# A graph-attention and FFN block on one core: one more projection by Strassen's algorithm, three mask columns in flight, and a bias moved

## The chip, the cores and the metric

The kernel runs on one core of a Trainium2 chip. The core has a matrix engine (TensorE, PE in the profile, with PEld for the loading of weights), a vector engine (VectorE, DVE), an activation engine (ScalarE, ACT), GpSimd (POOL) and SyncE (SP), which here only issues transfers. Transfers issued by one engine form a queue. The metric is device time in microseconds, the median of several runs.

## The reference

For x of 384 rows (nodes) and 1024 features:

```
h  = layernorm(x)
q  = h @ wq.T + bq;  k = h @ wk.T + bk;  v = h @ wv.T + bv
q2 = q @ wiq.T + biq; k2 = k @ wik.T + bik; v2 = v @ wiv.T + biv   # 16 heads of 64
mask = full(-inf); mask[src, dst] = softplus(etw)[type - 1]         # 12288 edges, the last one wins
mask[i, i] = softplus(etw)[3] where no edge is
a  = softmax(q2 @ k2.T / 8 + mask) @ v2                             # by head
x  = x + a @ wo.T + bo
h  = layernorm(x)
h  = silu(h @ w1 * s1) * (h @ w2 * s2);  h = gelu(h @ h1 * t1);  h = gelu(h @ h2 * t2)
x  = x + h @ w3 * s3
```

All weights of the attention are 1024 x 1024 in float32. The rows of a softmax sum to one, so a bias added to v2 comes out of the attention as the same bias.

## The kernel before

**Layout.** Activations are kept transposed where they are the input of a projection: xT, qT, vT, kT, q2T, k2T and aT have 8 tiles of 128 features by 384 nodes. v2 is kept with nodes in partitions (3 row tiles of 128 x 1024). Weights come as two halves of 2 MB each (512 output features), four buffers in all. A half's load can be issued only when the last product that reads the buffer's former contents is done. SP issues all of these loads and the other small ones in program order: a transfer that waits holds up all behind it.

**Order of work.** TensorE, VectorE, ScalarE and SP take their instructions strictly in the order in which the program names them; only GpSimd is left to the scheduler. The stages are: layernorm and transposes; q by plain matmuls (`project`, L378); q2, v and k by one level of Strassen's algorithm in the Winograd form (`project_fast`, L435); v2 by plain matmuls (L502 to L515); then k2 woven into the attention by heads (L556 and on), the output projection wo (L540), and the FFN.

**Strassen.** The weight is cut into quarters b11, b12, b21, b22 (b11 and b21 in the first half, b12 and b22 in the second) and the input into a11 to a22 (features by nodes). Four sums s1 to s4 of the input (`row_sums`) and four of the weight are made on VectorE: t3 = b22 - b12 (`third`, its own tile), b12 - b11 (`first`), then b11 + t3 (L459) and b21 minus that, all of them but t3 in place, 128 x 2048 elements each. Seven products m1 to m7 replace eight. The order on TensorE is: b11 with a11, t3 with s3, the new b11 with s2 (the third product), b21 with a12, b12 with s1, b22 with s4, the new b21 with a22. The call `beside[i]()` lets other work stand between the products in program order; `beside[0]` stands after the first product and ahead of b11 + t3.

**The mask table.** The edges are 96 columns of 128. A scatter (L355) writes one column's values into a table in DRAM, with an indirect transfer from GpSimd. So that the last edge wins, an entry whose cell occurs again later in the window of columns that can be in flight together is sent to a spare cell (`targets`, L333, on VectorE: for each column, a comparison of its keys with the keys of that and the following columns). DEEP = 2 columns are in flight: scatter i waits for scatter i - 2. `chunk()` does eight columns: it issues the load of the next eight columns' keys (`keys`, kr, on SP), makes the targets of its own eight, and issues eight scatters. After the last scatter the table is read back into nmask (L517), which the first step after the scores (L591, with the row's largest value) reads.

**Other places the change touches.** GpSimd adds the output bias bo to the residual xs after that (L523). The attention's product with v2 goes through a copy on ScalarE into aT (L621). For the FFN's weights the kernel tests whether they have low bits (`inspect`, L180, on ScalarE, sixteen pieces); the flag goes through a small matmul (L712) and a branch. `row` holds broadcast rows: biv and bo first, later the FFN's last scale in biv's place.

Of the kernel before, what the change touches and what calls it, by code (L numbers as in the profile page):

```python
# [30 lines left out]
DEEP = 2  # L31
# [12 lines left out]
def gnn_ffn_kernel(ctx: ExitStack, tc: tile.TileContext, x, edges, etw, vecs, rows,  # L44
# [34 lines left out]
    def load_rows(at, first, n):  # L79
        nc.sync.dma_start(row[:, at:at + n, :], bass.AP(  # L80
            tensor=rows.tensor, offset=rows.offset + first * F, ap=[[0, P], [F, n], [1, F]]))
# [98 lines left out]
    def inspect(raws):  # L180
        for raw in raws:
# [5 lines left out]
            nc.scalar.activation(low, low, AF.Copy, accum_out=lows[:, at:at + 1])  # L187
# [5 lines left out]
    with tc.tile_pool(name="edge", bufs=1) as ep, tc.tile_pool(name="krow", bufs=2) as krp, \  # L193
# [4 lines left out]
        tab = dram.tile([CELLS + DEEP * P, 1], FP, name="tab")  # L198
# [4 lines left out]
        for t in range(NT):  # L203
# [5 lines left out]
        nc.gpsimd.iota(spare, pattern=[[0, CHUNK // DEEP], [P, DEEP]], base=CELLS,  # L209
                       channel_multiplier=1, allow_small_or_imprecise_dtypes=True)  # L210
# [121 lines left out]

        def targets(c0, krf):  # L333

            for j in range(CHUNK):
                c = c0 + j
                w = min(DEEP, NCOL - c) * P
# [15 lines left out]
        def scatter(c0):  # L353
            for c in range(c0, c0 + CHUNK):
# [3 lines left out]
                for other in sent[-DEEP + 1:]:  # L358
                    tc.declare_no_dep(i, other, reason="no cell in common")
                if len(sent) >= DEEP:  # L360
                    after(i, sent[-DEEP])
# [34 lines left out]
        def row_sums(src, tag):  # L396

            sums = act.tile([P, 4, HK, HN], FP, tag=tag, name="sums")
            s1, s2, s3, s4 = (sums[:, i] for i in range(4))
            (a11, a12), (a21, a22) = ([src[:, k:k + HK, r:r + HN] for k in (0, HK)]  # L400
                                      for r in (0, HN))
# [10 lines left out]
        def third(at=0):  # L412

            b11, b12, b21, b22 = blocks(at)
            t3 = tp.tile([P, HK, FH], FP, tag="t3", name="t3")
            minus(t3, b22, b12)
            return t3
# [17 lines left out]
        def project_fast(src, sums, t3, dst, bias, beside):  # L435
# [3 lines left out]
            a11, a12, a22 = src[:, :HK, :HN], src[:, HK:, :HN], src[:, HK:, HN:]  # L439
# [41 lines left out]
        with tc.tile_pool(name="third", bufs=1) as tp, \  # L481
# [6 lines left out]
            sums_x = row_sums(xT, "k2T")  # L488
            chunk()
            load_rows(0, 0, 2)  # L490
# [4 lines left out]
            sums_q = row_sums(qT, "v2")  # L495
            t3s = []
            project_fast(qT, sums_q, t3, q2T, vec[:, BIQ:],
                         [nothing, chunk, chunk, lambda: t3s.append(third(2))])
            vT = act.tile([P, KF, N], FP, tag="t", name="vT", bufs=2)
            project_fast(xT, sums_x, t3s[0], vT, vec[:, BV:], [first, chunk, chunk, chunk])  # L500
            v2 = act.tile([P, NT, F], FP, tag="v2", name="v2")
            for half in range(2):  # L502
                (w,) = queue.pop(0)
                c = slice(half * FH, (half + 1) * FH)
                for t in range(NT):
                    ps = ps_st.tile([P, 512], FP, tag="st", name="ps")
                    for k in inputs:
                        nc.tensor.matmul(ps, lhsT=vT[:, k, t * P:(t + 1) * P], rhs=w[:, k, :],  # L508
                                         start=k == inputs[0], stop=k == inputs[-1])
                    nc.vector.tensor_add(v2[:, t, c], ps, row[:, 0, c])  # L510
                prefetch()
                for _ in range(2 - half):
                    chunk()
                if half == 0:
                    t3 = third(1)  # L515
            load_rows(0, 2, 1)
# [4 lines left out]
            for t in range(NT):  # L521
                tc.keep_in_program_order(
                    nc.gpsimd.tensor_add(xs[:, t, :], xs[:, t, :], row[:, 1, :]))  # L523
            kT = act.tile([P, KF, N], FP, tag="t", name="kT", bufs=2)
            project_fast(xT, sums_x, t3, kT, vec[:, BK:], [first, nothing, nothing, nothing])
# [6 lines left out]
    ps_ff = ctx.enter_context(tc.tile_pool(name="ps_ff", bufs=4, space=bass.MemoryType.PSUM))  # L532

# [16 lines left out]
    with tc.tile_pool(name="attn", bufs=1) as ap, \  # L550
# [62 lines left out]
        def weighted(pair):  # L613
# [7 lines left out]
            nc.scalar.copy(aT[:, pair, :], av[:, :N])  # L621
# [85 lines left out]
    for t in range(NT):  # L707
        st = small.tile([P, 2, 6], FP, name="st")
        add_out(multiply_out(t, 0), t, 0, st)
        if t == 2:  # L710
            fl = ps_mm.tile([P, 512], FP, tag="mm", name="fl")
# [3 lines left out]
            transpose_x2(1)  # L715
# [161 lines left out]
```

## Time and profile before

| | us |
|---|---|
| median of three runs (410.71 to 413.0) | 411.58 |
| the profiled execution | 408.51 |
| its span, first to last instruction | 406.5 |
| TensorE busy / VectorE / ScalarE / GpSimd | 389.9 / 211.4 / 106.3 / 123.3 |
| L508, v2's matmuls, 96 records, mean 0.592 each from start to end | 41.4 busy |
| L355, 96 scatters: busy, and idle before them | 108.0, 112.7 |
| of that idle, waiting for an earlier scatter to land | 66.2 |

A float32 matmul stands in the trace as two records. Matmuls overlap, so a record's length is longer than the step from one to the next; the sums here go by steps. PEclk is the clock that TensorE was granted: 1.00 is full speed. In the rows of the profile, L12 is line 12 of the kernel, out<-in are the tiles written and read, and what stands in square brackets is the idle time of the engine before the row and what ended it.

### The profile page before, as it was taken

To read this page: it belongs to the slowest core of one execution; us is meant where nothing else is said; L and a number is where in the kernel's file an instruction comes from. 1 tells how busy PE (TensorE), PEld (TensorE's weight loads), DVE (VectorE), ACT (ScalarE), POOL (GpSimd) and SP (SyncE) were. 2 spreads that over 40 slices of the span, in tenths; PEclk is the share of its full clock that TensorE was granted. 3 is DMA by queue.
4 is the path that set the end of the run, shared out by engine and by line. 5 is a ranking of instruction groups with operands and counts; after the bars stand their busy time and mean duration, and the time that the engine had idled before them with its cause. 6 is when DMAs were issued, how large, how long until landed. Compare 5 with 4: busy or idle time off the path is not lost.

```text
span 406.5 us, 4951 instructions
## 1 busy us (share of the span) xinstructions
PE 389.9 (96%) x1837; PEld 281.3 (69%) x1837; DVE 211.4 (52%) x611; ACT 106.3 (26%) x232; POOL 123.3 (30%) x117
## 2 busy tenths in 40 slices
PE   7899999999999999999999599999999999999993
PEld 6555589999997444699965255555544444699983
DVE  5638866857574145543510187676762045322455
ACT  4611110000000000010001176667762287132420
POOL 3022444655664464657725810000000000200000
PEclk9999999999999999999999879999999999999999
DMA  7599955048118335340291243111097040570004
GB/s 276 206 344 350 393 212 195 13 152 322 58 61 299 114 107 212 85 174 2 69 390 59 59 142 118 52 53 52 1 310 260 0 157 0 155 259 0 2 4 154
DMA packets 29353, 59.67 MB, mean 147 GB/s; under 512 B 4400, under 2 KB 7312, under 8 KB 29200
## 3 DMA queue, kind: packets, MB, share of 16 engines
q1 hardware_dynamic: 22160, 49.89, 34.1%
q0 software_dynamic: 6880, 9.03, 7.8%
q10 hardware_dynamic: 288, 0.41, 0.3%
q8 instruction: 16, 0.26, 0.3%
q14 instruction: 9, 0.07, 0.1%
HBM read 57.06 MB, written 2.26 MB: 146 GB/s over the span
## 4 chain that ended last, share of the span: by engine, by line
PE 69%; DMA 11%; POOL 8%; issue 4%; DVE 4%; ACT 3%; SPq 0%; POOLq 0%; ACTq 0%
PE ps L430 18%; PE ps L146 10%; DMA tab<-val,cell 10%; PE ps L540 8%; POOL tab L355 6%; PE ps L741 6%; PE ps L508 5%; PE ps L561 5%; PE pp L609 4%; PE av L618 4%; PE ps L753 4%; PE sc L577 4%; POOL xs L523 2%; ACT raw L187 1%; DMA xs<-in_x 1%
## 5 line engine op out<-in xcount | busy, mean ns | idle before, releaser
L355 POOL DMA_INDIRECT tab<-val,cell x96 | 108.0, 1125 | 112.7 <-DMA tab<-val,cell 66.2
L339 DVE SCALAR_TENSOR_TENSOR jk<-kr,key,jp 128x256 bf16<-128x256 f32 x96 | 39.8, 478 | 15.0 <-DMA kr<-keyd 15.0
L561 PE MATMUL ps<-kT,wik 128*128 128x384 f32 x128 | 44.6, 497 | 0.0
L540 PE MATMUL ps<-wo,aT 128*128 128x512 f32 x96 | 42.5, 593 | 0.0
L146 PE MATMUL ps<-xT,wq 128*128 128x384 f32 x128 | 41.5, 487 | 0.3 <-ACT xT L259 0.3
L508 PE MATMUL ps<-wiv,vT 128*128 128x512 f32 x96 | 41.4, 592 | 0.0
L591 DVE CUSTOM_DVE_ANT_0 e<-sc,nmask 128x384 f32<-128x384 f32 x48 | 23.9, 552 | 27.0 <-DMA nmask<-tab 25.4
L146 PEld LDWEIGHTS ps<-xT,wq 128*128 128x128 f32 x128 | 24.2, 190 | 17.2 <-ACT xT L259 0.5
L561 PEld LDWEIGHTS ps<-kT,wik 128*128 128x128 f32 x128 | 24.1, 196 | 14.9 <-issue 1.1
L593 ACT ACTIVATE e<-e,lo 128x384 f32<-128x384 f32 x48 | 28.9, 604 | 20.2 <-DVE lo L591 20.2
L508 PEld LDWEIGHTS ps<-wiv,vT 128*128 128x128 f32 x96 | 18.2, 190 | 22.5 <-issue 22.5
L540 PEld LDWEIGHTS ps<-wo,aT 128*128 128x128 f32 x96 | 17.7, 190 | 20.2 <-issue 20.2
L741 PE MATMUL ps<-x,w 128*128 128x384 f32 (+2 forms) x176 | 25.8, 307 | 0.0
L609 PEld LDWEIGHTS pp<-ident,e 128*128 128x128 f32 x144 | 16.7, 144 | 13.0 <-issue 5.6
L741 PEld LDWEIGHTS ps<-x,w 128*128 128x128 f32 x176 | 25.1, 190 | 0.5 <-issue 0.5
L577 PE MATMUL sc<-k2T,q2T 64*128 64x384 f32 x96 | 20.5, 529 | 4.9 <-DVE lo L591 4.9
L609 PE MATMUL pp<-ident,e 128*128 128x128 f32 x144 | 21.2, 284 | 0.8 <-POOL xs L523 0.8
L95 POOL DMA_DIRECT2D w<-in_w x3 | 2.6, 861 | 61.9 <-PE ps L561 60.0
L187 ACT ACTIVATE raw<-raw 128x1024 uint16<-128x1024 uint16 x16 | 21.1, 1342 | 0.0
L456 ACT COPY kT<-ps 128x384 f32<-128x384 f32 x2 | 1.0, 480 | 76.6 <-PE ps L430 76.6
L601 DVE TENSOR_SCALAR e<-e,rd 128x384 f32<-128x384 f32 x48 | 19.0, 438 | 0.9
L95 POOL DMA_DIRECT2D h<-in_h x2 | 1.5, 759 | 53.1 <-issue 53.1
(147 smaller groups left out, 551.1 us busy)
## 6 DMA issues: line engine op xcount, KB each, us to landing
kr<-keyd SPq DMA_DIRECT2D x11, 576.0 KB, 10.3
raw<-in_w SPq DMA_DIRECT2D x12, 512.0 KB, 5.2
w<-in_w POOLq DMA_DIRECT2D x3, 2048.0 KB
wiq<-in_wiq SPq DMA_DIRECT2D x2, 2048.0 KB, 17.9
wv<-in_wv SPq DMA_DIRECT2D x2, 2048.0 KB
wiv<-in_wiv SPq DMA_DIRECT2D x2, 2048.0 KB, 8.6
wk<-in_wk SPq DMA_DIRECT2D x2, 2048.0 KB
wik<-in_wik SPq DMA_DIRECT2D x2, 2048.0 KB
```

The lines of the kernel that those rows point to most:

```text
L146: nc.tensor.matmul(ps[:, :N], lhsT=w[:, k, o * P:(o + 1) * P], rhs=src[:, k, :], start=(k == 0), stop=(k == nk - 1))
L187: nc.scalar.activation(low, low, AF.Copy, accum_out=lows[:, at:at + 1])
L339: nc.vector.scalar_tensor_tensor(jk[:, :w], krf[:, j * P:j * P + w], key[:, c:c + 1], later[:, :w], op0=ALU.is_equal, op1=ALU.mult, accum_ ...
L355: i = nc.gpsimd.indirect_dma_start(out=tab, in_=val[:, c:c + 1], in_offset=None, out_offset=bass.IndirectOffsetOnAxis(ap=cell[:, c:c + 1], ...
L430: nc.tensor.matmul(ps[o // 2][:, o % 2, :HN], lhsT=w[:, k, o * P:(o + 1) * P], rhs=x[:, k, :], start=(o % 2, k) == (0, 0), stop=(o % 2, k) ...
L508: nc.tensor.matmul(ps, lhsT=vT[:, k, t * P:(t + 1) * P], rhs=w[:, k, :], start=k == inputs[0], stop=k == inputs[-1])
L540: nc.tensor.matmul(ps, lhsT=aT[:, k, t * P:(t + 1) * P], rhs=wos[half][:, k, :], start=k == 0, stop=k == KF - 1)
L561: nc.tensor.matmul(ps[:, :N], lhsT=wik[o // 4][:, k, o % 4 * P:(o % 4 + 1) * P], rhs=kT[:, k, :], start=k == inputs[0], stop=k == inputs[-1])
L577: nc.tensor.matmul(sc[:, :N], lhsT=q2T[r, pair, t * P:(t + 1) * P], rhs=k2T[r, pair, :], start=True, stop=True)
L593: nc.scalar.activation(e, e, AF.Exp, bias=lo, scale=-1.0, accum_out=dens[u][:, j:j + 1])
L609: nc.tensor.transpose(pt[:, m, :], e[:, m * P:(m + 1) * P], ident)
L741: nc.tensor.matmul(ps[:, rows], lhsT=w[:, k, o * P:(o + 1) * P], rhs=x[:, k, rows], start=n == 0, stop=n == len(todo) - 1)
```

## The change

- v2: row tiles 0 and 1 (256 nodes) go through Strassen's algorithm, with nodes as the stationary operand; row tile 2 by plain matmuls, from the weight's quarters before they are changed in place. Seven products of four matmuls each and two of eight. ScalarE copies three results out, VectorE does the rest.
- biv is no longer added to v2. It is loaded as a number per feature (a tile of 128 x 8, 4-byte elements each from its own place) and added in the copy into aT. Both other rows are loaded at once.
- Columns 0 to 31 of the table have three scatters in flight, the others two. The targets of the first columns compare 384 keys instead of 256, the keys' loads have ten columns instead of nine.
- One chunk moves: the q projection by Strassen now has a chunk in `beside[0]`, `[1]` and `[2]` (before in `[1]` and `[2]`); v has chunks in `[1]` to `[3]` as before, with a t3 for v2 ahead of the last; v2 has two chunks instead of three.
- bo is added to xs by VectorE, one row tile beside each of the last three places in k's projection.
- The low-bit test writes its copy to another tile; eight transposes stand ahead of the flag's matmul instead of behind it.

```diff
-DEEP = 2
+DEEP = 3
+FRONT = 32
...
-    def load_rows(at, first, n):
-        nc.sync.dma_start(row[:, at:at + n, :], bass.AP(
-            tensor=rows.tensor, offset=rows.offset + first * F, ap=[[0, P], [F, n], [1, F]]))
+    def load_rows():
+        nc.sync.dma_start(row, bass.AP(tensor=rows.tensor, offset=rows.offset + F,
+                                       ap=[[0, P], [F, 2], [1, F]]))
+        with nc.allow_non_contiguous_dma(reason="a number per feature"):
+            nc.sync.dma_start(biv, bass.AP(tensor=rows.tensor, offset=rows.offset,
+                                           ap=[[1, P], [P, KF]]))
...
-            nc.scalar.activation(low, low, AF.Copy, accum_out=lows[:, at:at + 1])
+            nc.scalar.activation(junk, low, AF.Copy, accum_out=lows[:, at:at + 1])
...
+        def flight(c):
+            return DEEP if c < FRONT else DEEP - 1
...
-                w = min(DEEP, NCOL - c) * P
+                w = min(flight(c + DEEP - 1), NCOL - c) * P
...
-                for other in sent[-DEEP + 1:]:
+                for other in sent[max(c - flight(c) + 1, 0):]:
                     tc.declare_no_dep(i, other, reason="no cell in common")
-                if len(sent) >= DEEP:
-                    after(i, sent[-DEEP])
+                for other in sent[max(c - DEEP, 0):max(c - flight(c) + 1, 0)]:
+                    after(i, other)
...
             project_fast(qT, sums_q, t3, q2T, vec[:, BIQ:],
-                         [nothing, chunk, chunk, lambda: t3s.append(third(2))])
+                         [chunk, chunk, chunk, lambda: t3s.append(third(2))])
...
-            project_fast(xT, sums_x, t3s[0], vT, vec[:, BV:], [first, chunk, chunk, chunk])
+            project_fast(xT, sums_x, t3s.pop(), vT, vec[:, BV:],
+                         [first, chunk, chunk, lambda: (t3s.append(third(2)), chunk())])
...
-            for half in range(2):
-                (w,) = queue.pop(0)
-                c = slice(half * FH, (half + 1) * FH)
-                for t in range(NT):
-                    ps = ps_st.tile([P, 512], FP, tag="st", name="ps")
-                    for k in inputs:
-                        nc.tensor.matmul(ps, lhsT=vT[:, k, t * P:(t + 1) * P], rhs=w[:, k, :],
-                                         start=k == inputs[0], stop=k == inputs[-1])
-                    nc.vector.tensor_add(v2[:, t, c], ps, row[:, 0, c])
-                prefetch()
-                for _ in range(2 - half):
-                    chunk()
-                if half == 0:
-                    t3 = third(1)
-            load_rows(0, 2, 1)
...
+            t3 = t3s.pop()
+            nc.scalar.copy(c11, block(a11, b11))
+            s1, s2, s3, s4 = row_sums(vT, P, tag="t", bufs=2)
+            nc.scalar.copy(v2[:, 2, :FH], last_tile(0))
+            chunk()
+            nc.vector.tensor_add(b11, b11, t3)
+            nc.scalar.copy(v2[:, 2, FH:], last_tile(1))
+            chunk()
+            minus(b12, b22, b11)
+            m7 = block(s3, t3)
+            m6 = block(s2, b11)
+            m2 = block(a12, b21)
+            add(c12, m6, c11)
+            add(c21, m7, c12)
+            add(c11, m2, c11)
+            minus(b21, b21, b11)
+            m5 = block(s1, b12)
+            add(c12, m5, c12)
+            add(c22, m5, c21)
+            t3 = third(2)
+            add(c12, block(s4, b22), c12)
+            add(c21, block(a22, b21), c21)
+            for _ in range(2):
+                queue.pop(0)
+                prefetch()
...
-            for t in range(NT):
-                tc.keep_in_program_order(
-                    nc.gpsimd.tensor_add(xs[:, t, :], xs[:, t, :], row[:, 1, :]))
+            biased = lambda t: lambda: nc.vector.tensor_add(xs[:, t, :], xs[:, t, :], row[:, 0, :])
...
-            project_fast(xT, sums_x, t3, kT, vec[:, BK:], [first, nothing, nothing, nothing])
+            project_fast(xT, sums_x, t3, kT, vec[:, BK:], [first, *(biased(t) for t in range(NT))])
...
-            nc.scalar.copy(aT[:, pair, :], av[:, :N])
+            nc.scalar.activation(aT[:, pair, :], av[:, :N], AF.Identity,
+                                 bias=biv[:, pair:pair + 1])
...
         if t == 2:
+            transpose_x2(1)
             fl = ps_mm.tile([P, 512], FP, tag="mm", name="fl")
...
             nc.vector.tensor_copy(flag, fl[:1, :1])
-            transpose_x2(1)
```

Here `block(x, w)` is four matmuls into one PSUM bank, `last_tile(half)` eight with the third row tile, `add` a VectorE sum of a bank and a part of v2.

## The prediction

> **What bounds the kernel now.** I read the page first, then the chain that ended last, then TensorE's, VectorE's and the DMA queue's instructions in order of time around each place that the diff touches. The page's busy rows say TensorE: PE is busy 96% of a 406.5 us span. The slices show the one hole (the 5, at 224 to 234 us) and that the granted clock fell with it.
>
> ```profile
> PE 389.9 (96%) x1837; PEld 281.3 (69%) x1837; DVE 211.4 (52%) x611; ACT 106.3 (26%) x232; POOL 123.3 (30%) x117
> PE   7899999999999999999999599999999999999993
> PEclk9999999999999999999999879999999999999999
> ```
>
> In the chain, TensorE carries everything up to 148 us with no gap. After that the chain runs along the mask table's scatters (L355) only because they end at the hole. So an edit is worth what it does to TensorE's stream: matmul time, holes, and clock.
>
> ```profile
> 13.03 41.52 PE ps L146 x128
> 54.55 72.80 PE ps L430 x448
> 127.35 20.61 PE ps L508 x48
> ```
>
> TensorE in time order around the hole (start, length, line, operands, count, idle before it):
>
> ```profile
> 225.92 0.92 PE L577 MATMUL sc<-k2T,q2T 64*128 64x384 f32 x4
> 231.70 2.12 PE L577 MATMUL sc<-k2T,q2T 64*128 64x384 f32 x4 [4.87 <-DVE lo L591]
> 234.62 1.51 PE L609 MATMUL pp<-ident,e 128*128 128x128 f32 x6 [0.79 <-POOL xs L523]
> 235.92 3.94 PE L561 MATMUL ps<-kT,wik 128*128 128x384 f32 x8
> 239.79 1.56 PE L577 MATMUL sc<-k2T,q2T 64*128 64x384 f32 x8
> ```
>
> The scores of unit 2 need a PSUM bank that L591 has to empty, and L591 waits for the mask (the wait list: 25.4 us, ended at 231.09). The same four score matmuls take 2.12 instead of 0.92.
>
> **Part 1, fewer matmuls in v2.** L508 issues 6 tiles x 8 = 48 fp32 matmuls of 128x512, which stand as 96 records. The first 48 records took 20.61 us, 0.429 each. After: the third row tile keeps 2 x 8, the two others take 7 products x 4, so 44, or 88 records of the same shape. 8 x 0.429 = **-3.4 us**, if operands are never late. Relative to the start of v2 TensorE does m1 (to 3.4), the third tile (to 17.2), m7, m6, m2 (to 27.4), m5, and two last. VectorE must fit: four sums of 512 elements (a 768 takes 0.96, so some 0.65 each), one chunk of targets (3.7), b11 plus t3 (2.29, after 10.3), a chunk (its keys come behind wk, at about 10.5) and b12 (2.28, after 17.2). b12 is done near 19.5 and wanted at 27.4: 8 us of cover. b21 is done near 30.5 and wanted at 34.3. A second t3 in the v projection (2.28) eats the 1.3 us for which VectorE waited before its last evictions, and 1 us more, hidden by m1 and half a tile. The three copies out on ACT (nearest row 0.58) have an idle engine.
>
> **Part 2, the mask and the bias off POOL.** Without the hole, from 225.92: eight score records 1.49, six transposes 0.72, eight L561 2.58 (the steady rows of the chain), so the next scores at 230.7 instead of 239.79: **-9.1 us**. That holds the idle time, the half clock, and the slow L601 pair (1.57 beside POOL's L523, 0.75 elsewhere). It needs the mask by 224.5 on the old clock: unit 0 must be normalised by 227.4, and L591, the exponential and L601 took 2.9 us from the mask on. The table: scatters fly 5.5 us while weights stream (24.74, 32.16, 39.26, 45.65 start the first pairs) and are 1.27 apart otherwise. Three in flight bring the first eight from four rounds of 7 us to under three, 8 us saved there and more by column 32. Against it: a scatter that meets a 2048-element VectorE op takes 3.09 instead of 0.97, and v2 adds four such ops, at most 8.4. I take the mask as 20 us earlier; part 4 shows that 0 would nearly do. The three bias adds become VectorE ops (about 1.2 each) in the k projection, where it idles 11.1 us before L450.
>
> **Part 3, small ones.** The flag's matmul L712 goes behind eight transposes that do not wait for it; from the last L540 to L712 TensorE lost 0.99 (0.83 of it in the row as idle), the transposes take 0.88: **-0.9**. The bias in aT makes an ACT copy of 0.464 into one of 0.58, 8 times 0.12, hidden behind L540 and L561 (if not: +0.9). The low-bit sums into another tile: same 1024 elements, 0.
>
> **Part 4, the moved chunk.** The old program calls nothing beside the first product of the q projection; the new one calls chunk there, ahead of b11 plus t3 on VectorE, which is strictly in program order (the new build has it so: eight target ops that wait for a DMA, then the 2048 add). Old order:
>
> ```profile
> 54.39 5.36 PE L430 MATMUL ps<-qT,wiq 128*128 128x192 f32 x32
> 59.59 5.36 PE L430 MATMUL ps<-sums,t 128*128 128x192 f32 x32
> 64.79 5.36 PE L430 MATMUL ps<-sums,wiq 128*128 128x192 f32 x32
> ```
> ```profile
> 59.79 2.29 DVE L459 TENSOR_TENSOR wiq<-wiq,t 128x2048 f32<-128x2048 f32 x1 [1.64 <-PE ps L430]
> 65.36 0.53 DVE L339 SCALAR_TENSOR_TENSOR jk<-kr,key,jp 128x256 bf16<-128x256 f32 x1 [3.28 <-DMA kr<-keyd]
> ```
> ```profile
> 54.58 0.38 SPq L95 DMA_DIRECT2D wv<-in_wv  x1
> 55.05 14.03 SPq L329 DMA_DIRECT2D kr<-keyd  x3
> ```
>
> The keys of this chunk stand on SP behind wv's second half, which waits for the q weights' buffer (54.5), so they land at 65.36. Nothing in the change brings them earlier. They get later: their rows are 10 instead of 9 (+0.3), and the new load of biv stands ahead on that queue. No row shows such a transfer. The Trainium skill (DMA: Bandwidth & Descriptors, Rules for kernel authors) has one descriptor per element for it: 1024, 64 for each of 16 engines. Floor: the 16-byte packets of wt last 9 ns, 0.6 us; ceiling: vec's 128 packets needed 0.76 us, 95 ns each per engine, 6.1 us. I take 3, between them, nearer to wt. The queue had room (DMA share 0.02 from 52.7 to 55.7), 3.0 less 0.6 for larger key rows before it, so 0.6 shows. Keys at 66.3, targets 3.70 (65.36 to 69.06), add 2.29: b11 is there at 72.3. The third product needs it at 64.79: **+7.5 us** of idle TensorE. Behind the add on VectorE wait chunk 5 and the sums out of PSUM; they keep their old distance to TensorE.
>
> Then the clock. Row: after the 4.87 us hole, TensorE's clock was 0.50 from 231.70 to 238.3.
>
> ```profile
> 231.70:234.62 2.92, 2.12 (x5) 1.01 (x5) 1.94 (x5) 1.31 (x4) 2.59 (x2) 0.50 0.01 3
> 234.62:238.30 3.68, 3.68 (x10) 2.65 (x11) 3.61 (x15) 2.94 (x10) 0.59 (x1) 0.50 0.00 0
> ```
>
> By this row a dense stream loses half of 6.6, 3.3 us. The Trainium skill (TensorE: Matmul & The Clock Gate, Part 1) has a free-running window of 3.4 us: one idle window halves the clock, one busy window restores it. So a dense stream is cold for 3.4 to 6.8 us after such a gap and loses 1.7 to 3.4. The sum would be -2.6 by the row, -3.3 by the middle of the rule. The row's hole was followed by a second idle piece (0.79), so I take the rule's middle: **+2.6**. While TensorE is 10 us later, the mask is wanted at 224.5 - 3.4 + 10.1 = 231.2: the old landing, 231.09, would do.
>
> **Sum.** -3.4 - 9.1 - 0.9 + 7.5 + 2.6 = -3.3 us. The profiled execution has 408.51 us for a span of 406.5 (2.0 around it), so 405.2. The median of the runs shown is 411.58, 3.1 above it. The table's 96 serial flights are what can vary most, and they leave the path; I give half of the 3.1 back: **406.6 us**. That an edit moves this kernel by 0.5% (2.1 us) is about what can be told from no change.
>
> **Rivals.**
> A, the forecast (0.68): 402.5 to 410.5 by the clock's 1.7 to 3.4, biv's 0.6 to 6.1 and the 3.1.
> B, no new wait (0.14): keys land early enough, or the wait is a fraction. For: other chunks found theirs landed. Against: the queue order and 65.36. Full gain: 408.51 or 411.58 less 13.4, 395 to 398; partial, about 401.
> C, slower (0.10): biv's short packets push wv and the keys back. Each us past 2.4 is a us of hole. Equal to before from a hole of 10.8, so biv of 6.3; slower by 0.5% from 8.4, 130 ns per descriptor. Against: the 95 ns ceiling. At 9 us: 414.
> D, the change does not do what it says (0.08): three in flight do not speed the table, or VectorE is late for v2's products. The first costs under 1 us (407.5), thanks to the hole at 65. The second: a hole of 3 us in v2 with its clock, 5 us, 411.6.
>
> **Numbers.** Faster: nine tenths of A, B, and half of D, 0.78; same, 0.15: the rest of A and part of C and D; slower 0.07, mostly C. Range 399.5 to 410.8: it leaves B's full gain and the worst of C and D outside, some 2 in 10. A's own range is 402.5 to 410.5.
>
> **What would show it.** TensorE: 7 to 8 us idle before the third product of the q projection, released by VectorE's 2048 add, half clock for 3.4 to 7 us after it, no other gap to the end of v2; 88 records of 128x512 in 37.7 us. VectorE: the targets' wait for keys now 8 us, ahead of the add. The mask lands well before the first scores, no wait of L591 for it. No gap before the flag's matmul. Wrong would be: third product on time (B); keys after 69 (C); a gap inside v2 or before the scores (D).

## The result, and the profile after

The changed kernel took 405.24 us (median of four runs, 404.39 to 406.64) against 411.52 for the kernel before (410.71 to 413.0): a ratio of 0.985, 95% interval 0.981 to 0.989, so 1.5% faster. The forecast was 406.6. The profiled execution of the changed kernel took 405.44 us for a span of 403.3; before it was 408.51 for 406.5. The sum of the prediction had 405.2 on that basis. All ratios here are to the kernel before on the same chip, and leave out executions that are more than 1.5% above the shortest of their kernel.

The page's rows of busy time and slices, as shown of the kernel before:

```profile
PE 386.7 (96%) x1829; PEld 281.8 (70%) x1829; DVE 230.4 (57%) x623; ACT 106.1 (26%) x235; POOL 119.5 (30%) x114
PE   7999994999999999999999999999999999999993
PEclk9999999699999999999999999999999999999998
```

The 5 in the 23rd slice, the hole at the mask, is gone. A 4 stands in the seventh slice, at 60 to 71 us, and the clock falls behind it. TensorE in time order around it, with the old third product at 64.79 for comparison (start, length, line, operands, count, idle time before it):

```profile
59.51 5.36 PE L444 MATMUL ps<-sums,t 128*128 128x192 f32 x32
71.35 8.08 PE L444 MATMUL ps<-sums,wiq 128*128 128x192 f32 x32 [6.47 <-DVE wiq L473]
79.26 5.36 PE L444 MATMUL ps<-qT,wiq 128*128 128x192 f32 x32
```

The third product starts 6.6 us late, and needs 7.91 us to the start of the next instead of 5.20. VectorE shows why it is late: the moved chunk waits for its keys, and the addition to b11 stands behind it (seven further compares and two small steps between them are left out).

```profile
65.33 0.48 DVE L350 SCALAR_TENSOR_TENSOR jk<-kr,key,jp 128x256 bf16<-128x256 f32 x1 [5.67 <-DMA kr<-keyd]
...
69.01 2.28 DVE L473 TENSOR_TENSOR wiq<-wiq,t 128x2048 f32<-128x2048 f32 x1
```

The granted clock over the hole, the slow product and the one after it (stretch, its length, busy time of PE, PEld, DVE, ACT and POOL, then the clock, the DMA share and GB/s):

```profile
64.71:71.35 6.64, 0.17 (x3) 0.01 (x1) 5.95 (x20) 0.00 (x0) 4.35 (x4) 0.89 0.33 57
71.35:79.26 7.91, 7.91 (x32) 7.91 (x33) 4.08 (x19) 0.00 (x0) 5.38 (x6) 0.66 0.38 142
79.26:84.46 5.20, 5.20 (x34) 5.20 (x33) 4.89 (x20) 0.00 (x0) 3.98 (x5) 1.00 0.02 2
```

At the other end, TensorE runs through the first scores without a gap:

```profile
226.20 0.92 PE L623 MATMUL sc<-k2T,q2T 64*128 64x384 f32 x4
227.05 4.78 PE L607 MATMUL ps<-kT,wik 128*128 128x384 f32 x14
231.76 1.56 PE L623 MATMUL sc<-k2T,q2T 64*128 64x384 f32 x8
233.25 0.88 PE L655 MATMUL pp<-ident,e 128*128 128x128 f32 x6
233.97 2.75 PE L607 MATMUL ps<-kT,wik 128*128 128x384 f32 x8
236.64 1.56 PE L623 MATMUL sc<-k2T,q2T 64*128 64x384 f32 x8
```

L637, the first step that reads the mask, still waits for it:

```profile
228.64 0.56 DVE L637 CUSTOM_DVE_ANT_0 e<-sc,nmask 128x384 f32<-128x384 f32 x1 [17.07 <-DMA nmask<-tab]
```

Most of these 17.07 us are not the mask's: VectorE has nothing to do ahead of L637, and the first scores, which L637 needs too, stood only at 227.1 (226.20 and 0.92). The mask cost L637 the last 1.5 us, in the kernel before 9.8 (scores at 221.3, mask at 231.1). TensorE felt nothing of the 1.5: the first unit of scores (two heads, one row tile) was normalised at 231.6, and its transposes were wanted at 233.25.

The mask came at 228.6, where it was 231.1 before: 2.5 us earlier, not 20. So two readings were open:

- **Exchange.** The hole at the mask went because TensorE comes there about 6 us later (9.3 by the new hole, less 3.4 by v2). The table's order alone did little in this kernel.
- **Two separate things.** The table is fast enough by itself, and the hole at 65 us is a plain loss of 9.3 us.

They differ in what happens when the new hole is taken out: 404 to 406 us by the first, 396 by the second.

### The profile page after: what moved, and what is told of

Read it like the earlier page. It is cut to its first block, busy times and chain, and to the rows that moved or that the text cites. A ratio compares the mean times of both kernels' runs of the same rounds, so it can differ in the third digit from the quotient of the medians.

```text
span 403.3 us, 4958 instructions
## 1 busy us (share of the span) xinstructions
PE 386.7 (96%) x1829; PEld 281.8 (70%) x1829; DVE 230.4 (57%) x623; ACT 106.1 (26%) x235; POOL 119.5 (30%) x114
## 4 chain that ended last, share of the span: by engine, by line
PE 79%; DMA 9%; DVE 8%; ACT 1%; issue 1%; POOL 0%; SPq 0%; DVEq 0%; ACTq 0%; POOLq 0%
PE ps L444 25%; PE ps L586 10%; PE ps L607 10%; PE ps L526 9%; PE ps L788 6%; DMA wiq<-in_wiq 5%; PE av L664 4%; PE sc L623 4%; PE pp L655 4%; PE ps L800 4%; DMA kr<-keyd 3%; DVE jk L350 3%; PE pw L234 1%; DVE y L883 1%; DVE y L882 1%; PE pt L737 1%
## 5 line engine op out<-in xcount | busy, mean ns | idle before, releaser
L366 POOL DMA_INDIRECT tab<-val,cell x96 | 110.9, 1156 | 104.9 <-DMA tab<-val,cell 58.2
L350 DVE SCALAR_TENSOR_TENSOR jk<-kr,key,jp 128x256 bf16<-128x256 f32 (+1 forms) x96 | 43.8, 520 | 11.8 <-DMA kr<-keyd 11.8
L607 PE MATMUL ps<-kT,wik 128*128 128x384 f32 x128 | 43.4, 487 | 0.0
L637 DVE CUSTOM_DVE_ANT_0 e<-sc,nmask 128x384 f32<-128x384 f32 x48 | 23.9, 553 | 18.9 <-DMA nmask<-tab 17.1
L607 PEld LDWEIGHTS ps<-kT,wik 128*128 128x128 f32 x128 | 23.4, 190 | 14.4 <-ACT k2T L610 0.5
L444 PE MATMUL ps<-sums,wiq 128*128 128x192 f32 x96 | 18.6, 361 | 6.5 <-DVE wiq L473 6.5
L526 PE MATMUL ps<-wiv,vT 128*128 128x512 f32 x56 | 24.5, 592 | 0.0
L444 PEld LDWEIGHTS ps<-sums,wiq 128*128 128x128 f32 x96 | 18.2, 215 | 6.8 <-DVE wiq L473 6.8
L526 PEld LDWEIGHTS ps<-wiv,vT 128*128 128x128 f32 x56 | 10.6, 190 | 12.9 <-issue 12.2
L623 PE MATMUL sc<-k2T,q2T 64*128 64x384 f32 x96 | 19.0, 511 | 0.0
```

Source lines behind the costliest of these rows:

```text
L350: nc.vector.scalar_tensor_tensor(jk[:, :w], krf[:, j * P:j * P + w], key[:, c:c + 1], later[:, :w], op0=ALU.is_equal, op1=ALU.mult, accum_ ...
L366: i = nc.gpsimd.indirect_dma_start(out=tab, in_=val[:, c:c + 1], in_offset=None, out_offset=bass.IndirectOffsetOnAxis(ap=cell[:, c:c + 1], ...
L444: nc.tensor.matmul(ps[o // 2][:, o % 2, :HN], lhsT=w[:, k, o * P:(o + 1) * P], rhs=x[:, k, :], start=(o % 2, k) == (0, 0), stop=(o % 2, k) ...
L526: nc.tensor.matmul(ps, lhsT=x, rhs=w, start=i == 0, stop=i == len(steps) - 1)
L607: nc.tensor.matmul(ps[:, :N], lhsT=wik[o // 4][:, k, o % 4 * P:(o % 4 + 1) * P], rhs=kT[:, k, :], start=k == inputs[0], stop=k == inputs[-1])
L623: nc.tensor.matmul(sc[:, :N], lhsT=q2T[r, pair, t * P:(t + 1) * P], rhs=k2T[r, pair, :], start=True, stop=True)
```

## The experiments

Twelve kernels ran, in three groups of four on three chips. Some traces of the second and third group have stretches in which TensorE waits for nothing that the profile shows (the last section), so there the stages say more than the total.

Stages are read from TensorE's rows: the first matmul of v2, the first of k2 (kT with wik) and the first of the FFN. From k2 to the FFN everything that waits for the mask is inside. "Mask read" is when GpSimd issued the transfer of the table into nmask; the mask landed 4.3 to 4.6 us later where that can be read, but 8.3 in the first run that put three columns in flight throughout. The moved chunk stands ahead of the addition to b11 or behind it.

| kernel | columns in flight | moved chunk | v2 | v2 starts | k2 starts | FFN starts | k2 to FFN | mask read |
|---|---|---|---|---|---|---|---|---|
| before | 2 | behind | plain | 127.2 | 204.8 | 351.8 | 147.1 | 226.5 |
| changed | 3, then 2 | ahead | Strassen | 136.5 | 210.6 | 348.1 | 137.5 | 224.1 |
| e1 | 3, then 2 | behind | Strassen | 127.2 | 201.4 | 344.9 | 143.5 | 221.4 |
| e2 | 3, then 2 | ahead, keys early | Strassen | 127.2 | 201.4 | 345.6 | 144.2 | 221.1 |
| e3 | 3, then 2 | behind | plain | 127.3 | 204.9 | 346.6 | 141.7 | 222.7 |
| e4 | 3 | behind | Strassen | 127.7 | 201.9 | 339.4 | 137.5 | 206.2 |
| e5 | 2 | ahead | plain | 136.9 | 214.5 | 352.5 | 138.1 | 227.6 |
| e6 | 2 | ahead | Strassen | 136.8 | 217.0 | 355.5 | 138.4 | 229.2 |
| e7 | 3 | behind | plain | 128.0 | 210.9 | 348.1 | 137.2 | 196.2 |
| e8 | 3, then 2 | ahead, hole filled | Strassen | 138.8 | 216.1 | 353.6 | 137.5 | 218.1 |
| e9 | 3, then 2 | ahead, hole filled | Strassen | 148.0 | 222.2 | 359.7 | 137.5 | 216.1 |
| e10 | 3 | ahead | Strassen | 137.1 | 212.9 | 350.4 | 137.5 | 202.7 |
| e11 | 3 | behind | Strassen | 128.4 | 212.3 | 349.8 | 137.5 | 200.0 |
| e12 | 2 | behind | Strassen | 127.3 | 201.4 | 356.3 | 154.9 | 232.2 |

137.5 us, or 138.1 with the attention of the kernel before, is this stage when nothing waits for the mask.

### The chunk put back (e1)

```diff
             project_fast(qT, sums_q, t3, q2T, vec[:, BIQ:],
-                         [chunk, chunk, chunk, lambda: t3s.append(third(2))])
+                         [nothing, lambda: (chunk(), chunk()), chunk, lambda: t3s.append(third(2))])
```

> The changed kernel with the first stage of the second q projection left as it was before (no chunk ahead of b11+t3); the chunk that stood there is done in the second stage, so that the number of chunks stays. Both theories: the third product of the q projection starts at about 64.7 us instead of 71.35, the next one 5.2 us later, and v2 starts at about 127.2 instead of 136.5. Theory 1 (the two holes are exchanged: the mask itself is only 2.5 us earlier than in the kernel before, and TensorE's lateness is what hides it): the attention's first wait for the mask comes back, with 5 to 8 us of idle TensorE near 221 to 229 and 2 to 3 us of half clock after it; time within 1.5 us of the changed kernel, 404 to 406.5. Theory 2 (the hole at 65 us is a plain loss and the mask is early by itself): no idle time at the mask, and the whole 9.3 us are gained, about 396.

Measured: 402.40 us, ratio 0.980 (0.976 to 0.983). The new hole is gone and v2 starts 9.2 us earlier, as both theories had it. TensorE's rows at the mask:

```profile
222.54 0.92 PE L623 MATMUL sc<-k2T,q2T 64*128 64x384 f32 x4
226.51 1.39 PE L623 MATMUL sc<-k2T,q2T 64*128 64x384 f32 x4 [3.05 <-DVE lo L637]
228.60 1.51 PE L655 MATMUL pp<-ident,e 128*128 128x128 f32 x6 [0.70 <-DVE e L647]
229.91 3.59 PE L607 MATMUL ps<-kT,wik 128*128 128x384 f32 x8
```

The hole at the mask is back: 3.75 us idle, and half clock in parts (eight L607 records take 3.59 instead of 2.75). The stage costs 143.5 instead of 137.5. Of the 9.2 us taken out ahead of the mask, 6.0 came back there; the spans differ by 3.2 (403.3 to 400.1). Exchange, then, but not one for one: its band of 404 to 406.5 missed by 1.6. The mask itself was also read 2.7 us earlier here, which is the likely reason for the miss; what made it earlier was not tested.

### The keys first (e2)

```diff
             load_rows()
+            krs.append(keys(4 * CHUNK))
...
-            if c0 + CHUNK < NCOL:
+            if c0 + CHUNK < NCOL and len(krs) < 2:
```

> The changed kernel with one DMA moved: the keys of the fifth chunk are sent for before the first weight of wv instead of behind wv's second half; the chunk stays ahead of b11+t3 on VectorE. Both theories: the wait for the keys (5.67 us) is gone; what is left of the hole is the chunk's own work on VectorE, about 8 operations of 0.48 us and the cell arithmetic, 1 to 4 us of delay of the third product, if any. Theory 1: what is gained there comes back as a wait for the mask near 224 to 229 us, time 403.5 to 406.5. Theory 2: the gain stays, 397 to 400.

Measured: 402.68 us, ratio 0.978 (0.974 to 0.982). The chunk itself costs TensorE nothing. Its compares start at 58.07 instead of 65.33, and the addition to b11 ends before the third product wants it:

```profile
58.07 0.48 DVE L350 SCALAR_TENSOR_TENSOR jk<-kr,key,jp 128x256 bf16<-128x256 f32 x1
...
61.73 2.28 DVE L473 TENSOR_TENSOR wiq<-wiq,t 128x2048 f32<-128x2048 f32 x1
```

So the whole of the new hole was the keys' place on SP's queue. The rest goes as in the run before: 144.2 us from k2 to the FFN. TensorE's idle time at the mask is one piece of 2.90 us here, and the clock is at 0.50 for 6.8 us behind it: 6.7 us in all.

### Three in flight alone (e3)

The kernel before, with the table's order of the changed one.

```diff
-DEEP = 2
+DEEP = 3
+FRONT = 32
...
-                for other in sent[-DEEP + 1:]:
+                for other in sent[max(c - flight(c) + 1, 0):]:
```

> The kernel before, with only the table's order changed: three mask columns in flight for the first 32, two behind them. Everything else is the kernel before. Theory 1: the mask lands about 2 to 5 us earlier than at 231.1 and the hole at 226 to 240 us shrinks by the same amount; 406.5 to 409.5 against 411.5. My forecast's step (the table 20 us earlier): the hole is gone altogether, with its half clock, 9.1 us: about 402.5.

Measured: 400.50 us, ratio 0.974 (0.970 to 0.977). This single part does more than the whole change. The mask was earlier by 3.8 us only, as the first theory had it; the time fell by more than it had. The rows at the mask:

```profile
226.06 0.92 PE L582 MATMUL sc<-k2T,q2T 64*128 64x384 f32 x4
227.84 1.38 PE L582 MATMUL sc<-k2T,q2T 64*128 64x384 f32 x4 [0.86 <-DVE lo L596]
230.82 0.85 PE L614 MATMUL pp<-ident,e 128*128 128x128 f32 x6 [1.60 <-DVE e L606]
231.51 2.75 PE L566 MATMUL ps<-kT,wik 128*128 128x384 f32 x8
```

Idle time is 2.5 us here instead of 5.7, and the clock stayed at 1.00:

```profile
226.90:231.51 4.61, 2.15 (x13) 1.30 (x12) 3.31 (x10) 1.31 (x4) 3.59 (x2) 1.00 0.00 2
231.51:236.00 4.49, 4.49 (x21) 2.35 (x20) 4.42 (x18) 4.44 (x11) 0.95 (x1) 1.00 0.38 84
```

Two pieces of idle, 0.9 and 1.6 us, cost 3.6 in the stage; one of 4.9 with 0.8 behind it cost 9.0. The difference between the profiled spans is 5.3 us (406.5 to 401.2). The medians differ by more, 10.7: the kernel before has a mean granted clock of 0.980 to 0.986 over its timed runs against 0.990 in its profile, and this one 0.996 to 0.999. With a span of 409 us and 0.982, 7.4 us' worth of full clock is missing, with 398 and 0.996 only 1.6; the two profiles lack 4.1 and 0.4. So the clock explains about 2 of the 5.4 us by which the medians differ more than the spans. The other 3 or so (this kernel's profiled execution, 403.24, is also its longest) no trace shows.

### Three in flight throughout (e4)

```diff
-FRONT = 32
+FRONT = 128
```
on top of the chunk put back. (The table has 96 columns; 128 only stands for "all".)

> As the run with the chunk put back, and three mask columns in flight for all 128 instead of the first 32. Theory 1 (the table sets the mask's time, and holes are exchanged as long as it is late): the table ends 5 to 12 us earlier, at 207 to 214; if the mask lands by about 221, both holes are gone and the time is 395 to 398; if it lands later, each us late costs one. Theory 2 (the mask is early anyway): the same as the run with the chunk put back. A third possibility: three in flight make each column's descriptors slower as much as they overlap, so that the last column is sent no earlier than 217, and the hole at the mask stays as in that run.

Measured: 396.61 us (396.07 to 397.28), ratio 0.965 (0.962 to 0.969). It beats both kernels, the changed one by 8.6 us. No hole is left: from 75.61 to 381.48 us the chain that ended last is TensorE's, but for a stretch at 279 to 284 us through VectorE and ScalarE.

```profile
217.46 0.92 PE L623 MATMUL sc<-k2T,q2T 64*128 64x384 f32 x4
218.30 4.78 PE L607 MATMUL ps<-kT,wik 128*128 128x384 f32 x14
223.02 1.56 PE L623 MATMUL sc<-k2T,q2T 64*128 64x384 f32 x8
```

The scatters say where the changed kernel lost what it had won. Start of the scatter of each column, us:

| column (from 0) | 32 | 48 | 64 | 80 | 95, the last |
|---|---|---|---|---|---|
| before | 106.6 | 138.5 | 166.1 | 192.5 | 223.8 |
| changed: three to column 31, then two | 90.9 | 125.5 | 158.9 | 189.8 | 219.1 |
| three throughout, chunk behind | 90.7 | 119.3 | 149.8 | 178.3 | 199.6 |

At column 32 the changed kernel leads by 15.7 us, at the last by 4.7. With three throughout the lead grows to 24. So the front of the table was sped up, and the lead melted behind it, while two columns were in flight. Late targets were not what held it: those of the last chunk were ready at 152.8 us, and its first scatter started at 202.2. From column 32 to the last the changed kernel took 128.2 us, the kernel before 117.2; 7.3 of the 11 us are longer waits between scatters, 3.9 longer scatters.

### The chunk moved in the kernel before (e5)

```diff
-                         [nothing, chunk, chunk, lambda: t3s.append(third(2))])
+                         [chunk, chunk, chunk, lambda: t3s.append(third(2))])
...
-                for _ in range(2 - half):
-                    chunk()
+                chunk()
```

> The kernel before, with only the chunk moved: one chunk ahead of b11+t3 in the second q projection, one fewer behind v2's first half. Both theories: the third product starts 6 to 7.5 us later (71 to 72.5) and at half clock, v2 at about 136.5. Theory 1, exchange: TensorE comes to the mask about 9 us later, the mask lands where it did or a little earlier (229 to 231), and the idle time and half clock at 226 to 240 go; the time does not rise: 408 to 411.5. Rival, plain sum: the hole at 65 us is added to the kernel before, and the wait for the mask moves on with it: 418 to 421.

Measured: 412.54 us as the median of four runs (408.4, 408.9, 416.2 and 418.1); the ratio, 0.990 (0.982 to 0.998), is of the first two. The clearest case of exchange is the profiled execution: a new hole of 7.23 us, v2 9.7 us later, and 408.89 against 408.51. The mask read was issued 1.1 us later than before, TensorE came to it 9.7 us later, and there was no gap at it:

```profile
72.08 7.76 PE L430 MATMUL ps<-sums,wiq 128*128 128x192 f32 x32 [7.23 <-DVE wiq L459]
...
230.04 0.92 PE L576 MATMUL sc<-k2T,q2T 64*128 64x384 f32 x4
230.89 4.78 PE L560 MATMUL ps<-kT,wik 128*128 128x384 f32 x14
235.60 1.56 PE L576 MATMUL sc<-k2T,q2T 64*128 64x384 f32 x8
```

A hole that cost 9.7 us with its clock left the time as it was. The plain sum, 418 to 421, is out for the profiled execution; the two long runs have no trace. GpSimd's three additions of bo stand here as in the kernel before (228.4 to 235.4 us), so they alone don't make the hole at the mask.

### The table undone in the changed kernel (e6)

```diff
-FRONT = 32
+FRONT = 0
```

> The changed kernel with two mask columns in flight throughout, as in the kernel before; all else is the changed kernel. Theory 1: the mask lands 2 to 5 us later than at 228.6, which its 1.7 us of slack only half cover: TensorE waits 0.5 to 3.5 us at the mask[...], 405.5 to 408.5. My forecast's step (three in flight bring the table 20 us): the mask lands near 248 and the time is over 415.

Measured: 412.05 us, ratio 0.997 (0.991 to 1.004). The mask read was issued 5.1 us later than in the changed kernel, just above the first theory's 2 to 5. In the profiled execution k's projection took 6.0 us longer than its 36.4, waiting for nothing shown, so TensorE came late to the mask and did not wait for it (no gap at the scores); the total can't be split between the two. An estimate from the rows: TensorE of the changed kernel could have taken the mask by 230.3 (228.6 and 1.7 to spare), and here it would have landed at about 233.6 (229.2 and 4.4). So without the 6.0 us some 3 us of waiting would have come back.

### Plain v2 where nothing waits for the mask (e7)

The kernel with three in flight throughout, with v2 by the loop of the kernel before (three copies per half on ScalarE, no bias).

```diff
-            c11, c12, c21, c22 = (v2[:, t, c:c + FH] for t in (0, 1) for c in (0, FH))
...
+                    for k in inputs:
+                        nc.tensor.matmul(ps, lhsT=vT[:, k, t * P:(t + 1) * P], rhs=w[:, k, :],
+                                         start=k == inputs[0], stop=k == inputs[-1])
+                    nc.scalar.copy(v2[:, t, c], ps)
```

> The kernel with three in flight for all columns and the chunk put back, with v2 of the first two row tiles by plain products as in the kernel before: 8 more matmuls of 128 x 512. There nothing waits for the mask. If a matmul taken away is worth its time where TensorE sets the end: 8 x 0.43 = 3.4 us more, 400.0 against 396.6. If Strassen's additions on VectorE, which stand among the chunks, cost as much as it saves: 396 to 397.5.

Measured: 402.76 us, ratio 0.976 (0.969 to 0.983). In the chains, v2 takes 41.20 us for 96 records here against 37.77 for 88 in the kernel with Strassen's v2, 3.43 more:

```profile
128.12 41.20 PE ps L527 x96
```
```profile
127.88 37.77 PE ps L526 x88
```

The other 5.3 us of the difference in span (402.8 against 394.1) are stretches in k's projection without a shown cause; the two runs of 400.7 and 400.9 are 4.2 above the kernel with Strassen's v2, which ran on another chip. So the eight matmuls are worth their 3.4 us where TensorE sets the end.

### The hole filled (e8, e9)

Idle matmuls ahead of the third product, first 36, which was twice too many (each is two records), then 18. Nothing reads them.

```diff
+            if fill:
+                ps = ps_mm.tile([P, 512], FP, tag="mm", name="ps")
+                for i in range(fill):
+                    nc.tensor.matmul(ps[:, :HN], lhsT=t3[:, 0, :P], rhs=s3[:, 0, :],
+                                     start=i == 0, stop=i == fill - 1)
             m6 = product(b11, s2)
```

> The changed kernel with 36 further matmuls of 128 x 192 ahead of the third product of the q projection, whose result nothing reads: they keep TensorE at work in the hole of 6.6 us, for about 5.9 us of it. If the half clock behind the hole comes of its idle time: the third product takes 5.2 us instead of 7.9 and v2 starts at 133.8 instead of 136.5; at the mask 1.7 us of slack are used up and about 1 us of waiting comes back: 403 to 404, 1.2 to 2.2 under the changed kernel's 405.24. If the product is slow for another reason (what VectorE or the DMAs do beside it): 7.9 us as before and 405 to 406.

> As the run with the hole filled, with half the filling: 18 matmuls of 128 x 192, which are 36 records of 0.1625 us, 5.9 us in a hole of 6.6. If the half clock behind the hole comes of the idle time: the third product starts at 71.35 as in the changed kernel and takes 5.2 us instead of 7.9, v2 starts at 133.9 instead of 136.6; the mask then has no slack left and about 1 us of waiting comes back: 403 to 404 against 405.24. If the clock is cut for another reason: product 7.9 us, 405 to 406.

Measured: 411.14 us with 36, ratio 0.995 (0.988 to 1.002), and 416.55 with 18, a median of twenty runs from 405.1 to 436.7; its ratio, 0.990 (0.983 to 0.996), is of two of them. The totals say nothing of the clock: in the second trace TensorE stood still in pieces from 85 to 99 us. The third product says it plainly. With 18:

```profile
65.00 6.01 PE L478 MATMUL ps<-sums,t 128*128 128x192 f32 x36
71.87 5.47 PE L444 MATMUL ps<-sums,wiq 128*128 128x192 f32 x32 [0.86 <-DVE wiq L473]
77.18 5.36 PE L444 MATMUL ps<-qT,wiq 128*128 128x192 f32 x32
```

It starts 0.5 us later than in the changed kernel, and takes 5.31 us to the next product instead of 7.91, at a clock of 1.00 (the columns are those of the clock's rows above):

```profile
71.87:77.18 5.31, 5.31 (x33) 5.31 (x33) 4.01 (x19) 0.00 (x0) 4.09 (x5) 1.00 0.27 80
```

VectorE, GpSimd and the DMAs went on beside it. With 36 it takes 5.20. The 2.7 us behind the hole come of TensorE's idling and of nothing beside it.

### The hole kept, the table fast (e10)

The changed kernel with three in flight throughout.

```diff
-FRONT = 32
+FRONT = 128
```

> The changed kernel with three mask columns in flight for all 128 and nothing else, so that the hole ahead of the third product stays. Exchange: the mask lands 5 to 12 us earlier than at 228.5, but in the changed kernel TensorE does not wait for it, so nothing is gained: 404.5 to 406.5, the wider compares of the chunk ahead of b11+t3 (0.61 against 0.52 us for each of 8) making the hole about 0.7 longer. If the mask is still a limit of the changed kernel in some way that the trace hides: 396 to 402.

Measured: 407.46 us, ratio 0.984 (0.972 to 0.996), an interval that holds the changed kernel's 0.985. The mask read was issued at 202.7, 21 us earlier than in the changed kernel, and the stage that reads it took 137.5 us as there. Three in flight throughout gain nothing behind the hole, and 5.8 us without it (402.40 to 396.61, the chunk put back in both). The hole was 7.50 us, 1.0 more for the wider compares.

### The residual's bias on GpSimd (e11)

The kernel with three in flight throughout, with bo added as before.

```diff
-            biased = lambda t: lambda: nc.vector.tensor_add(xs[:, t, :], xs[:, t, :], row[:, 0, :])
+            for t in range(NT):
+                tc.keep_in_program_order(
+                    nc.gpsimd.tensor_add(xs[:, t, :], xs[:, t, :], row[:, 0, :]))
...
-            project_fast(xT, sums_x, t3, kT, vec[:, BK:], [first, *(biased(t) for t in range(NT))])
+            project_fast(xT, sums_x, t3, kT, vec[:, BK:], [first, nothing, nothing, nothing])
```

> The kernel with three in flight for all columns and the chunk put back, with the bias of the residual added on GpSimd as in the kernel before (three additions behind the mask's DMA) instead of on VectorE. In the kernel before TensorE waited 0.8 us behind these additions, beside the mask's wait. If that was a part of the mask's wait: 396 to 397.3, no difference from 396.6. If the additions cost on their own: 0.8 to 3 us more.

Measured: 409.33 us, ratio 0.989 (0.980 to 0.998). The total is above both expectations, but k's projection alone took 46 us instead of 36.4 in pieces without a cause, 9.7 of the 10.0 us between the profiled spans (404.1 against 394.1). From k2 to the FFN it took 137.5 us, as with the bias on VectorE. That stage shows no price for either engine once the mask is early; a difference of less than 1 us in the total is not settled. With the mask late GpSimd has one: where its additions run beside the first pair's normalising on VectorE, that takes 1.65 us (e3) or 1.57 (the kernel before), and 0.75 in the changed kernel.

### Table and chunk both undone (e12)

```diff
-FRONT = 32
+FRONT = 0
```
on top of the chunk put back.

> The changed kernel with both undone: two mask columns in flight throughout, and the chunk behind the third product as before. What stays of the change is Strassen's v2, the output bias, the flag and the bias on VectorE, so the mask is as late as in the kernel before and TensorE comes to it 3.4 us earlier. Exchange: the mask lands at 229 to 232, TensorE waits for it 7 to 9 us at falling clock, and the 3.4 us of v2 are turned into waiting: 409.5 to 412.5. If matmuls taken away count in full: 407 to 408.

Measured: 411.00 us, ratio 0.997 (0.994 to 1.000). What is left of the change here, Strassen's v2 with the smaller parts, brings nothing that can be told from no change. The profiled execution is the longest of the twenty, 413.69; its hole at the mask:

```profile
222.57 0.92 PE L623 MATMUL sc<-k2T,q2T 64*128 64x384 f32 x4
237.37 2.12 PE L623 MATMUL sc<-k2T,q2T 64*128 64x384 f32 x4 [13.88 <-DVE lo L637]
239.46 1.51 PE L655 MATMUL pp<-ident,e 128*128 128x128 f32 x6
240.76 4.15 PE L607 MATMUL ps<-kT,wik 128*128 128x384 f32 x8
```

TensorE comes to k2 3.4 us earlier than in the kernel before (201.4 against 204.8), and waits longer in this execution: 154.9 us from k2 to the FFN. The mask read was also 5.7 us later than before, which the forecast of 229 to 232 did not have.

## Why the prediction was right, and where it was not

The time was right, and all five terms were within 0.9 us of what the profiled execution shows. One step behind them was wrong: the reason for the largest term. So the mechanism was half right: the holes and the clock came as forecast, the table did not.

| term | forecast | profile |
|---|---|---|
| v2's eight matmuls | -3.4 | 41.20 to 37.77: -3.43, no gap inside |
| the hole at the mask | -9.1 | from the second unit's scores to the fourth's, 13.87 (225.92 to 239.79) to 4.88 (231.76 to 236.64): -9.0 |
| the flag's matmul behind the transposes | -0.9 | from the transposes for the FFN's first row tile to the branch, 16.25 to 15.40: -0.85 |
| the new hole | +7.5 | 71.35 less 64.71: +6.64 |
| half clock after it | +2.6 | 7.91 less 5.20: +2.71 |
| sum | -3.3 | span -3.2 |

The rows do not quite add up to the span (-3.9): 0.3 went to a wait of the attention's transposes for ScalarE at 292, 0.5 to the last output, which took longer to land behind the last work of the engines.

**The step that failed.** "I take the mask as 20 us earlier; part 4 shows that 0 would nearly do." The first half is wrong: it was 2.5. The second half is what happened. The forecast had the first 32 columns faster, as they were (15.7 us at column 32), and took the lead as kept. It was not: behind column 31 the rule of two in flight is the old one, and by the last column 4.7 us were left; three throughout kept it. The line "The mask lands well before the first scores, no wait of L591 for it" was wrong with it: the mask came at 228.6, 1.5 us after the first scores. The -9.1 stood because the new hole, which the forecast counted as a loss beside it, is also what made it true. The two terms were no independent items, as part 4's last sentence half saw (with TensorE 10 us later, "the old landing, 231.09, would do"). That the largest term came out right is in this sense luck: by the forecast's own reason, a table 20 us earlier, it would have stood without the new hole, and there it does not (e1). The runs show it from both sides: with the hole alone (e5) the mask's hole goes, with the hole taken out (e1, e2) it comes back, and behind the hole a table 21 us faster is worth nothing (e10).

**The new hole, 0.9 too large.** The step was "Keys at 66.3". They landed at 65.33, as before (65.36). biv's load was taken as 3 us, of which 0.6 were to show, and 0.3 were added for wider rows of keys. Neither showed: SP issued biv at 36.62, it had landed by 51.5, and SP issued the keys at 54.98 (55.05 before), behind the same wait for a buffer. Rival C, a slow biv, is out with it. VectorE's wait for the keys was 5.67 us, where the forecast named 8.

**The clock, right.** 2.71 against 2.6. The row of the old hole said 3.3; the estimate from the free-running window of 3.4 us that the Trainium skill states (TensorE: Matmul & The Clock Gate, Part 1) had its middle at 2.6, which was nearer. That it hit within 0.1 is luck: the same product lost 3.09 us in e6, 2.39 in e5 and 2.06 in e10, all within the estimate's 1.7 to 3.4, and not in the order of their holes (6.46, 7.23 and 7.50 us). In the changed kernel the clock was at 0.50 from 69.86 to 76.69 us; the product started at 71.35, so 5.34 us of it fell into that stretch. These stretches fit the page's window: 3.41 us in e1, twice that here, three times in e6. Filling the hole took the loss away altogether (e8, e9).

**Half of the 3.1.** The forecast gave back half of what the median of the kernel before lies above its profiled execution. The changed kernel's median (405.24) lies 0.2 below its own profiled execution: all of it went. (405.2 and half of 3.1 also make 406.8, not 406.6.)

**What the parts are worth.** By themselves: three in flight 0.974 (e3), the moved chunk 0.990 (e5, from two runs; by the profiles no change), Strassen's v2 with the small parts 0.997 (e12); together 0.985. The three do not add up, since the first takes the mask's hole out from one side and the other two move TensorE against it in opposite directions. The moved chunk is a loss as soon as the table is early: 0.985 with it, 0.980 without (e1), and with three throughout 0.984 with it (e10) and 0.965 without (e4). Strassen's v2 is worth 3.4 us where nothing waits for the mask (e7 against e4) and nothing measurable where something does (e12). The kernel with the table's order alone (e3) had a lower median than the one with Strassen's v2 added (e1), 400.5 against 402.4; their profiled spans stand the other way, 401.2 and 400.1, so which is faster is not shown.

What stays open: why the lead melts as far as it does. That scatters behind column 31 wait for the landing of the one before the last is the rule of the code, and more in flight cures it; late targets are out (e4's section). How much of it is Strassen's additions on VectorE, and how much the weight loads that the earlier scatters meet, was not told apart. With plain v2 and three throughout the mask read was issued at 196.2, with Strassen's v2 at 200.0 to 206.2; with two in flight and the chunk ahead 227.6 and 229.2.

## What to carry to other kernels

Two waits on the same engine are one account: a hole early on hides a late transfer further down, so before a hole is counted as a loss, or a transfer as a gain, ask at what time the engine will come to the next wait and when what it waits for is there. Price a wait by its length and by the clock: 2.5 us of idle in two short pieces cost 3.6 at full clock, one piece of 2.9 cost 6.7 and one of 4.9 with 0.8 behind it 9.0, both with the clock at half behind them. A pipeline that was made deeper only at its start lost 11.0 of its 15.7 us of lead in the rest (changed kernel); look at its last element, not at where the deep part ends.

## What the runs showed that was not expected

- **Stretches with no cause.** In six of the eight traces of the second and third chip TensorE stands still in pieces of 0.2 to 1.5 us, with nothing to wait for by the profile ("issue"): five times in k's projection, which takes 1.6 to 9.7 us longer for it, and once, in the kernel with 18 idle matmuls, at 85 to 99 us. In the six traces of the changed kernel, the kernel before and the first chip there is none. From the run with the bias on GpSimd:

```profile
190.04 1.03 PE L444 MATMUL ps<-sums,wk 128*128 128x192 f32 x3 [0.28 <-issue]
192.14 0.48 PE L444 MATMUL ps<-sums,wk 128*128 128x192 f32 x2 [1.07 <-issue]
...
196.35 0.48 PE L444 MATMUL ps<-sums,wk 128*128 128x192 f32 x1 [0.61 <-issue]
```

  In this run the pieces add up to 4.4 us; the clock was at 0.50 from 193.06 to 203.30 us, which makes up most of the rest of the 9.7. The cause is open. It is why totals of the second and third group were not compared with those of the first beyond their ratios.
- **The low-bit sums.** The same 128 x 1024 elements took 1.06 us instead of 1.34 on ScalarE once their copy went to a bf16 tile instead of back in place as uint16. Which of the two does it was not tried.
- **The mask's transfer.** It landed 4.3 to 4.6 us after issue in the kernels with the mask late, but 8.3 where it was issued at 206 us (e4), beside a weight load: the DMA engines were busy for 0.91 of that stretch, for 0.49 of the 4.3 us in the changed kernel.
